# The output stage of a two-layer state-space kernel: how the column-wise scans are added in, and on which engines the norm's sums run

## The chip, the cores and the metric

The kernel runs on one core of one Trainium2 chip. The metric is the device time of one execution in microseconds (us); the time of a kernel is the median of its runs. A profile of one further execution gives the trace from which single durations come.

## What is computed

The input is a batch of four 128x128 images with 192 channels, float32. Layer 0 (projection, depthwise convolution, one scan over the pixels, three dilated convolutions, a norm, an output projection) is not touched. Layer 1 is a two-dimensional selective scan: the image is projected, convolved, and scanned in four orders k = 0 to 3 (by rows forward and backward, by columns forward and backward). What matters here comes after the scans:

```python
y0 = ys[0].reshape(B, C, H, W)
y1 = ys[1][..., ::-1].reshape(B, C, H, W)
y2 = jnp.transpose(ys[2].reshape(B, C, W, H), (0, 1, 3, 2))
y3 = jnp.transpose(ys[3][..., ::-1].reshape(B, C, W, H), (0, 1, 3, 2))
y = y0 + y1 + y2 + y3
y = jnp.transpose(y, (0, 2, 3, 1))
mu = y.mean(-1, keepdims=True)
var = y.var(-1, keepdims=True)
y = (y - mu) / jnp.sqrt(var + 1e-05) * ln_g + ln_b
y = y * jax.nn.silu(z)
return y @ out_w
```

So the column-wise results have to be turned (width and height exchanged) before they meet the row-wise ones; then come a norm over the 192 channels of each pixel, a gate with silu(z), and an output projection. z is a projection of the layer's input, which is also added to the result.

## The kernel before

Four stages follow each other: the transposition of the input, layer 0, the convolution of layer 1 (`in_conv`, whose lines L933 to L959 the prediction also reads), the scans (`scans`), and the output stage (`outputs`). In layer 1 two images form a pair (PAIRS = 2), and their 2 x 192 channels lie in three blocks of 128 partitions: block 0 holds channels 0 to 127 of the first image, block 2 those of the second, block 1 the last 64 channels of both, one image in each half. A chunk is 8 image rows, T = 1024 pixels; there are 16 chunks (NCH) for each pair.

**The order of the work.** Each stage writes its operations to a list (`op`) with an engine, an assumed cost, what they read and write, and for some a shift in the list (`early`). `Order.emit` plays the list through once at build time, with these costs, and so fixes the order of the instructions on each engine; the engines then keep that order and wait for one another where data or buffers ask for it. `keep` is the penalty for an operation that needs another activation table than the one loaded, `idle` the wait that is accepted before another operation is preferred. A buffer (`buf(tag, bufs, ...)`) names its ring and how many tiles the ring has.

**The scans.** For each pair, each order k and each chunk there are six groups m of 64 channels with eight units each. A unit is an exponential on ACT (`dA`, L1244), a scan on DVE (L1250), a product on POOL (`hc`, L1256) and a matmul that sums over states (`Y`, L1264). After eight units `finish` adds the sum to what the earlier order left (`prev`; L1286, L1290 or L1292 by k) and stores it: `y[0]` holds the row-wise sum, `y[1]` the column-wise sum, whose pixels are in column order. There is one `Y` bank and there are two `y` tiles.

**The output stage** has two parts. `merge(p, i)` loads a whole 128x128 image of the column-wise block (`img`, L1377, four parts of 2 MB), then for each chunk loads the row-wise block (`m`, L1384), adds the turned view of the image to it on DVE (L1388, reading `img` with a step of one column) and stores the sum back (L1394). All three blocks of pair 0 are merged ahead of its first chunk; those of pair 1 are placed at chunks 1, 6 and 11 of pair 0. `chunk(p, j)` does the rest for 8 rows:

- load three y blocks (L1403) and three blocks of the layer's input (`x`, L789);
- average over channels on PE (`averages`): for each of two images a 128-row matmul (L1424) and a 64-row matmul for its half of block 1 (L1429), into a PSUM tile of two banks. It is called twice, first for the mean (called M here), then for the mean square (V);
- subtract the mean on DVE (L1437), square on ACT (L1441), V, then Ln (L1446) and Exp (L1450) on ACT give the reciprocal root;
- scale by it on DVE (the norm, L1453);
- for each block project the input to z (`pair_project`, L828), Silu on ACT (L1462), add the bias and gate on DVE (L1465);
- the output projection O in two halves of four image rows: 128-row matmuls with the gated y (L1479) and with an identity for the input itself (L1482), then the 64-row ones (L1488, L1493), row by row; ACT copies the result out (`ot`, L1500) and SP stores it (L1505).

PSUM holds three tiles `f` for averages and O and one tile `z`. y and x have two tiles for each block, the squares `s` one, the output `ot` one for each image. POOL has no work in this stage. 64-row matmuls on the two halves of the partitions [...]can run side by side; a block's matmuls here alternate between 128-row and 64-row form.

Of the kernel before, what the change touches and what calls it, by code (L numbers as in the profile page):

```python
# [16 lines left out]
B, H, W, C = 4, 128, 128, 192  # L17
L = H * W
R = 8
# [24 lines left out]
DILS = (5, 3)  # L44
NEAR = [(t, t // 3 - 1, t % 3 - 1) for t in range(9) if t != 4]
# [37 lines left out]
class Order:  # L83
# [32 lines left out]
    def emit(self):  # L116
# [14 lines left out]
        while len(order) < len(ops):  # L131
# [55 lines left out]
            for m in after[n]:  # L187
                left[m] -= 1
                ready_at[m] = max(
                    ready_at[m], done + (0.0 if e == ops[m][0] and not size else self.HOP)  # L190
                )
                if not left[m] and m < high:
                    ready[ops[m][0]].append(m)
        for n in order:
            for b in ops[n][4]:
                b()
            ops[n][2]()
# [3 lines left out]
class Maker:  # L201
# [784 lines left out]
    def scans(self, xc, delta, cs, y, w, ident, alog, dsum, dtb2):  # L986
# [22 lines left out]
        with ExitStack() as ctx:  # L1009
# [261 lines left out]
            def finish(m):  # L1271
# [12 lines left out]
                def add():  # L1284
                    if k == 0:
                        nc.vector.scalar_tensor_tensor(  # L1286
                            t(), prev[m](), dsum[:, hf : hf + 1], ym(), ALU.mult, ALU.add
                        )
                    elif k == 2:
                        nc.vector.tensor_copy(t(), ym())  # L1290
                    else:
                        nc.vector.tensor_tensor(t(), prev[m](), ym(), ALU.add)  # L1292

                def store():
                    for th, a in enumerate(y_part(y[k // 2][p][i], m)):
                        nc.sync.dma_start(a, t()[64 * th : 64 * th + 64])
# [55 lines left out]
    def outputs(self, y, x1T, gn, out, win, wo, vec, ident, eps):  # L1352
# [4 lines left out]
        with ExitStack() as ctx:  # L1357
            p1 = ctx.enter_context(tc.tile_pool(name="s_1", bufs=1))
            ps = ctx.enter_context(tc.tile_pool(name="s_ps", bufs=3, space=PSUM))
            psZ = ctx.enter_context(tc.tile_pool(name="s_psZ", bufs=1, space=PSUM))  # L1360
# [3 lines left out]
            od = Order(keep=167, idle=1.550, rate=300e3)  # L1364
            op = od.op

# [3 lines left out]
            def bank2(stream):  # L1370
                return buf("f", 3, 128, 2, 512, pool=ps, stream=stream)

            def merge(p, i):
                img = buf("img", 1, 128, W, H)
                for c in range(4):
                    ws = slice(c * W // 4, (c + 1) * W // 4)
                    op("SP", 0.1, lambda ws=ws: nc.sync.dma_start(  # L1377
                        img()[:, ws].rearrange("p w h -> p (w h)"),
                        y[1][p][i][:, ws.start * H : ws.stop * H],
                    ), reads=[img], writes=[(img, c)], size=2.1e6, early=-243)  # L1380
                for j in range(NCH):
                    cols = slice(j * T, (j + 1) * T)
                    t = buf("m", 3, 128, T)
                    op("SP", 0.11, lambda t=t, cols=cols: nc.sync.dma_start(  # L1384
                        t(), y[0][p][i][:, cols]), writes=[t], size=524e3, early=-438)

                    def add(t=t, j=j):
                        nc.vector.tensor_tensor(  # L1388
                            rows(t()), rows(t()),
                            img()[:, :, R * j : R * (j + 1)].rearrange("p w r -> p r w"), ALU.add,  # L1390
                        )

                    op("DVE", 1.9, add, reads=[img, *((img, c) for c in range(4))], writes=[t], early=-723)
                    op("SP", 0.12, lambda t=t, cols=cols: nc.sync.dma_start(  # L1394
                        y[0][p][i][:, cols], t()), reads=[t], writes=[("y", p, i, j)], size=524e3, early=-216)

            def chunk(p, j):
                terms, bias = pw[p]
                cols = slice(j * T, (j + 1) * T)
                ys, x1, sq = [], [], []  # L1400
                for i in range(3):
                    yt, xt = buf(f"y{i}", 2, 128, T), buf(f"x{i}", 2, 128, T)
                    op("SP", 0.1, lambda yt=yt, i=i: nc.sync.dma_start(yt(), y[0][p][i][:, cols]),  # L1403
                       reads=[("y", p, i, j)], writes=[yt], size=524e3, early=765)
                    op("SP", 0.13, lambda xt=xt, i=i: self.load_block(xt(), x1T, p, i, cols),
                       writes=[xt], size=524e3)
                    ys.append(yt)
                    x1.append(xt)
                    sq.append(buf(f"s{i}", 1, 128, T))
# [7 lines left out]
                def averages(name, src):  # L1417
                    gs = [bank2(name), bank2(name)]

                    def mm():  # L1420
                        for h in range(2):
                            c = slice(512 * h, 512 * h + 512)
                            for e in range(2):
                                nc.tensor.matmul(  # L1424
                                    gs[e]()[:, h], avg, src[2 * e]()[:, c], start=True, stop=False
                                )
                            for e in range(2):
                                k = slice(64 * e, 64 * e + 64)
                                nc.tensor.matmul(  # L1429
                                    gs[e]()[:, h], avg[k], src[1]()[k, c], start=False, stop=True  # L1430
                                )

                    op("PE", 4.4, mm, reads=src, writes=gs, early=57)
                    return gs

                gm = averages("M", ys)
                by_batch(lambda e, i, k: op("DVE", 1.23, lambda: nc.vector.tensor_tensor(  # L1437
                    ys[i]()[k], ys[i]()[k], flat(gm[e]())[k], ALU.subtract),
                    reads=[gm[e]], writes=[ys[i]]))
                for i in range(3):  # L1440
                    op("ACT", 1.08, lambda i=i: nc.scalar.activation(sq[i](), ys[i](), AF.Square),  # L1441
                       reads=[ys[i]], writes=[sq[i]])
                gv = averages("V", sq)
                rs = [buf("rs", 2, 128, T) for _ in range(2)]
                for e in range(2):
                    op("ACT", 1.13, lambda e=e: nc.scalar.activation(  # L1446
                        rs[e](), flat(gv[e]()), AF.Ln, bias=eps),
                        reads=[gv[e]], writes=[rs[e]], table="ln")
                for e in range(2):
                    op("ACT", 1.1, lambda e=e: nc.scalar.activation(  # L1450
                        rs[e](), rs[e](), AF.Exp, scale=-0.5),
                        writes=[rs[e]], table="exp")
                by_batch(lambda e, i, k: op("DVE", 1.24, lambda: nc.vector.scalar_tensor_tensor(  # L1453
                    ys[i]()[k], ys[i]()[k], vec[k, i % 2, V1_G : V1_G + 1], rs[e]()[k],
                    ALU.mult, ALU.mult), reads=[rs[e]], writes=[ys[i]], early=-540))
                for i in range(3):
                    gz, sz = buf("z", 1, 128, 2, 512, pool=psZ), buf("sz", 2, 128, T)
                    op("PE", 3.0, lambda i=i, gz=gz: self.pair_project(
                        [gz()[:, h] for h in range(2)], i, terms,
                        lambda src, h: x1[src]()[:, 512 * h : 512 * h + 512],  # L1460
                    ), reads=x1, writes=[gz])
                    op("ACT", 1.05, lambda i=i, gz=gz, sz=sz: nc.scalar.activation(  # L1462
                        sz(), flat(gz()), AF.Silu, bias=bias[:, i : i + 1]),
                        reads=[gz], writes=[sz], table="silu")
                    op("DVE", 1.25, lambda i=i, sz=sz: nc.vector.scalar_tensor_tensor(  # L1465
                        ys[i](), ys[i](), vec[:, i % 2, V1_B : V1_B + 1], sz(),
                        ALU.add, ALU.mult), reads=[sz], writes=[ys[i]])
                ot = [buf(f"ot{e}", 1, 128, R, C) for e in range(2)]
                for h in range(2):
                    go = [bank2("O"), bank2("O")]  # L1470

                    def mm(h=h, go=go):
                        for r in range(4):
                            tok = slice((4 * h + r) * W, (4 * h + r + 1) * W)
                            dst = [
                                go[e]()[:, r // 2, (r % 2) * C : (r % 2 + 1) * C] for e in range(2)
                            ]
                            for e in range(2):
                                nc.tensor.matmul(  # L1479
                                    dst[e], ys[2 * e]()[:, tok], wo[:, 0], start=True, stop=False  # L1480
                                )
                                nc.tensor.matmul(  # L1482
                                    dst[e][:, 0:128], x1[2 * e]()[:, tok], ident,
                                    start=False, stop=False,
                                )
                            for e in range(2):
                                k = slice(64 * e, 64 * e + 64)
                                nc.tensor.matmul(  # L1488
                                    dst[e], ys[1]()[k, tok], wo[k, 1 + e], start=False, stop=False
                                )  # L1490
                            for e in range(2):
                                k = slice(64 * e, 64 * e + 64)
                                nc.tensor.matmul(  # L1493
                                    dst[e][:, 128:C], x1[1]()[k, tok], ident[k, k],
                                    start=False, stop=True,
# [210 lines left out]
```

## Time and profile before

| what | value |
|---|---|
| median of 3 runs | 26036.89 us (26029.69 to 26136.25) |
| the profiled execution | 26124.05 us, span 26122.3 us |
| busy in the span: PE, DVE, ACT, POOL | 91%, 84%, 80%, 79% |
| output stage, first image load to the end | 24528 to 26122 us |
| DVE merge add, L1388, 128x1024 | 96 times, mean 1.92 us |
| DVE subtraction L1437, norm L1453, gate L1465 | mean 1.21, 1.28, 1.28 us |
| ACT square, Ln, Exp, Silu, copy to `ot` | mean 1.05, 1.11, 1.05, 1.11, 0.80 us |
| ACT table load | mean 1.28 us |

The page gives busy time over the whole span; the groups by line give how often an instruction ran and how long one took; the chain of waits follows the work that ended last back from the end; the order of time lists single instructions. A row of the groups or of the order of time names line, engine, operation, output and inputs. A float32 matmul appears as two records. "Granted clock" is the share of TensorE's full clock.

### The profile page before, as it was taken

The page shows a single profiled execution, that of the slowest core. Times are in us where ns is not written, and L with a number is a line of the kernel's source. Part 1 is how long each engine was busy: PE and PEld are TensorE (multiplying, and loading weights), DVE is VectorE, ACT ScalarE, POOL GpSimd, SP SyncE. Part 2 cuts the span into 40 slices and gives each one's busy share as a digit, 9 for nine tenths or more (in the row PEclk, how much of TensorE's full clock was granted, in tenths as well). Part 3 has the DMA queues.
Part 4 walks back from the last instruction along what each step waited for, and adds up shares of the span by engine and source line. Part 5 has one row for each costly group of instructions (what it writes and reads, how often), then busy time and mean ns, then how long its engine had stood idle before and what let it go on. Part 6 is the DMA issues. An engine that isn't in the chain of part 4 may idle for free.

```text
span 26122.3 us, 435536 instructions
## 1 busy us (share of the span) xinstructions
PE 23658.7 (91%) x168196; PEld 8704.1 (33%) x168196; DVE 21934.3 (84%) x15400; ACT 20802.7 (80%) x24211; POOL 20539.1 (79%) x9962
## 2 busy tenths in 40 slices
PE   4999999998899999999999999999999999999699
PEld 2333232322233333333333333333333333333245
DVE  3889888888788989888898889888988898888643
ACT  5999998966688888888887878888888888888443
POOL 3999998955588888888888888888888888888400
PEclk6999999999899999999998989999999999999799
DMA  6998889876545455444444545444544444544563
GB/s 205 248 248 251 245 249 244 248 213 208 155 127 134 131 136 136 131 124 120 122 126 127 134 124 137 129 129 132 135 132 132 116 124 118 134 128 130 189 229 107
DMA packets 1646421, 4171.84 MB, mean 160 GB/s; under 512 B 236800, under 2 KB 387776, under 8 KB 1641280
## 3 DMA queue, kind: packets, MB, share of 16 engines
q1 hardware_dynamic: 1644352, 4143.97, 57.0%
q8 instruction: 1333, 21.84, 0.4%
q14 instruction: 736, 6.03, 0.1%
HBM read 3203.95 MB, written 939.10 MB: 159 GB/s over the span
## 4 chain that ended last, share of the span: by engine, by line
PE 43%; DVE 19%; ACT 12%; issue 6%; DMA 4%; POOL 4%; SPq 1%; DVEq 0%; POOLq 0%; ACTq 0%
DVE h L1250 14%; PE f L1217 13%; PE Y L1264 10%; ACT h L1228 6%; ACT dA L1244 3%; PE s L1071 3%; PE hf L615 3%; POOL hc L1256 2%; PE s L1094 2%; PE z L828 1%; DMA C<-cs 1%; DVE D L1143 1%; DVE acc L939 1%; PE f L723 1%; PE g L706 1%
## 5 line engine op out<-in xcount | busy, mean ns | idle before, releaser
L1256 POOL TENSOR_TENSOR hc<-h,C 128x1024 f32<-128x1024 f32 x6144 | 14344.0, 2366 | 2340.8 <-PE Y L1264 1133.0
L1250 DVE TENSOR_TENSOR_SCAN h<-dA,st,h 128x1024 f32<-128x1024 f32 x5760 | 13128.7, 2331 | 746.4 <-ACT st L1280 300.2
L1228 ACT COPY h<-f 128x1024 f32<-128x1024 f32 (+3 forms) x8192 | 6334.4, 799 | 2176.4 <-PE f L1217 2109.6
L1217 PE MATMUL f<-D,dT 32*64 32x256 f32 x98304 | 7138.7, 407 | 782.8 <-ACT h L1228 638.0
L1264 PE MATMUL Y<-hc,sel 128*64 128x512 f32 x24576 | 6967.1, 654 | 477.1 <-POOL hc L1256 222.0
L1244 ACT ACTIVATE dA<-d,alog 128x1024 f32<-128x1024 f32 x6144 | 6904.6, 1124 | 308.8 <-DVE h L1250 254.3
L1217 PEld LDWEIGHTS f<-D,dT 32*64 32x64 f32 x98304 | 3270.7, 137 | 6657.9 <-ACT h L1228 4793.7
L495 POOL TENSOR_TENSOR xs<-xs,pr 128x1024 f32<-128x1024 f32 x1536 | 3641.6, 2373 | 233.5 <-ACT pr L490 160.4
L635 DVE SCALAR_TENSOR_TENSOR hf<-hh,vec,hf 128x512 f32<-128x512 f32 x3072 | 2315.2, 754 | 232.2 <-PE hf L615 134.3
L1264 PEld LDWEIGHTS Y<-hc,sel 128*64 128x64 f32 x24576 | 1318.8, 141 | 2971.1 <-issue 1794.2
L615 PE MATMUL hf<-sa,diag 96*32 96x512 f32 x18432 | 2173.9, 610 | 78.8 <-DVE y L646 40.3
L1143 DVE TENSOR_TENSOR D<-s,mask 128x1024 f32<-128x1024 f32 x1024 | 1238.2, 1209 | 865.4 <-PE s L1137 865.4
L490 ACT ACTIVATE pr<-xi,vec 128x1024 f32<-128x1024 f32 x1536 | 1703.7, 1142 | 174.6 <-POOL xs L495 171.7
L615 PEld LDWEIGHTS hf<-sa,diag 96*32 96x32 f32 x18432 | 553.4, 110 | 1599.4 <-issue 1340.0
L1104 POOL TENSOR_TENSOR u<-l,u 128x1024 f32<-128x1024 f32 x384 | 908.4, 2366 | 164.7 <-ACT l L1097 139.2
L1250 DVE TENSOR_TENSOR_SCAN h<-dA,h 128x1024 f32<-128x1024 f32 x384 | 856.5, 2273 | 63.6 <-ACT dA L1244 31.4
L1094 PE MATMUL s<-pj,w 128*128 128x512 f32 x1536 | 901.3, 670 | 6.3 <-ACT l L1097 2.0
L1097 ACT ACTIVATE l<-s,vec 128x512 f32<-128x512 f32 x768 | 528.0, 687 | 345.2 <-PE s L1094 340.7
L1071 PE MATMUL s<-u,w 128*128 128x512 f32 x1536 | 743.2, 621 | 53.8 <-DMA prev<-xc 53.0
L706 PE MATMUL g<-xz,w 96*128 96x512 f32 x1536 | 764.2, 622 | 26.6 <-DVE y L715 14.0
L1137 PEld LDWEIGHTS s<-ident,pj 128*128 128x128 f32 x4096 | 550.0, 195 | 595.0 <-issue 255.1
L939 DVE SCALAR_TENSOR_TENSOR acc<-xi,vec,acc 128x1024 f32<-128x1024 f32 x384 | 715.9, 1864 | 26.9
(208 smaller groups left out, 21228.3 us busy)
## 6 DMA issues: line engine op xcount, KB each, us to landing
C<-cs SPq DMA_DIRECT2D x4096, 256.0 KB, 4.8
sa<-hpad SPq DMA_DIRECT2D x2304, 276.0 KB, 6.2
d<-delta SPq DMA_DIRECT2D x1536, 256.0 KB, 4.2
u<-xc SPq DMA_DIRECT2D x384, 512.0 KB, 4.7
delta<-l SPq DMA_DIRECT2D x384, 512.0 KB, 3.8
y<-y SPq DMA_DIRECT2D x1536, 128.0 KB, 3.3
hh<-hpad SPq DMA_DIRECT2D x384, 414.0 KB, 6.3
hpad<-hp SPq DMA_DIRECT2D x192, 552.0 KB, 6.7
```

What stands on the lines that cost most here:

```text
L490: op("ACT", 1.1, lambda pr=pr, t=t: nc.scalar.activation(rows(pr()), x()[:, t // 3 : t // 3 + R, t % 3 : t % 3 + W], AF.Copy, scale=v(k, V ...
L495: op("POOL", 2.38, lambda pr=pr: nc.gpsimd.tensor_tensor(o(), o(), pr(), ALU.add), reads=[pr], writes=[o], early=-390)
L615: nc.tensor.matmul(o()[32 * g : 32 * g + 32], diag[:, d, s, k, g], x[:, g, :, c0 : c0 + W], start=(d == 0 and s == 0), stop=(d == 1 and s ...
L635: nc.vector.scalar_tensor_tensor(o3, hh()[:, 1 + dy : 5 + dy, PAD + dx : PAD + dx + W], v(k, V0_K + col), o3, ALU.mult, ALU.add,)
L1071: nc.tensor.matmul(g(), wt()[:, 0, i], uu[i]()[:, 512 * c : 512 * c + 512], start=(i == 0), stop=(i == 2),)
L1143: nc.vector.tensor_tensor(t().rearrange("t a (n s) -> t (a n) s", s=32), g()[:, : 2 * NS].unsqueeze(2).to_broadcast([128, 2 * NS, 32]), ma ...
L1217: nc.tensor.matmul(gs()[64 * jn : 64 * jn + 64, n, 256 * a : 256 * a + 256], td()[rt, r // 64, 2 * sb + a], tD()[rt, a, 256 * jn : 256 * j ...
L1228: nc.scalar.copy(H[:, at : at + nq, 256 * sb : 256 * sb + 256].rearrange("p q (a r s) -> p q a r s", a=2, s=32)[:, :, :, 2 * rp : 2 * rp + 2],
L1244: op("ACT", 1.16, lambda: nc.scalar.activation(a(), d(), AF.Exp, scale=alog[:, c : c + 1]), reads=[d], writes=[a], table="exp", early=-522)
L1250: nc.vector.tensor_tensor_scan(hs[:, way], a()[:, way], hs[:, way], 0.0 if at == 0 else s0()[:, q : q + 1], ALU.mult, ALU.add,)
L1256: op("POOL", 2.4, lambda: nc.gpsimd.tensor_tensor(t(), hs, tC(), ALU.mult), reads=[hq, tC], writes=[t])
L1264: nc.tensor.matmul(ym()[64 * th : 64 * th + 64], sel, t()[:, 512 * th : 512 * th + 512], start=(q == 0), stop=(q == NQ - 1),)
```

## The change

The edit has five parts, four of them in the output stage.

1. **Turned groups.** For k = 3 (the last of the column orders) `finish` writes its sum in another order: within each tile the four columns of 128 pixels are split in four groups of TG = 32 image rows, and the store goes to a new scratch tensor `yt`, laid out by group, then column, then row. A store has 256 runs of 512 bytes instead of 64 of 2 KB.
2. **Addition chunk by chunk.** `merge` and `img` are gone. Every fourth chunk loads for each block the next 32-row group of `yt` (2 MB, ring of two); each chunk loads its y blocks from `y[0]` as the scans left them, and DVE adds the turned view of the group in place. There is no write-back.
3. **Norm sums partly on GpSimd.** POOL adds block 1's half to block 0 or block 2 (64 partitions by 1024), and copies the other half, ahead of M; it adds the squares likewise ahead of V. Each average is then 128-row matmuls alone, two for each image.
4. **Paired matmuls.** The z projections of blocks 0 and 2 are issued together, first all 128-row ones, then the 64-row ones of both images in pairs; block 1's projection is as before. O likewise: in each half first all 128-row matmuls of four rows, then all 64-row ones. PSUM has four `f` tiles and no `z` tile.
5. **New list order.** A subclass `Timed` of `Order` makes the list with other costs, a model of the TensorE clock, of the change of tiling mode and of the way between engines, and with shifts by kind of operation (`OUT_EARLY`) in place of the shifts at each operation.

The order of all instructions ahead of the output stage is the same as before, but for the form of the add and the store of part 1.

```diff
+TG = 32
+OUT_KEEP, OUT_IDLE = 520, 2.009
+OUT_EARLY = {'oh': -4, 'ln': 51, 'o': -32, 'ot': -4, 'silu': -9, 'turned': -50, 'V': -3, 'out': -74, 'x': -130, 'merge': 32, 'sum': -42, 'sqs': -157, 'rs': -137, 'norm': -8, 'gate': 343}
...
+class Timed(Order):
+    WINDOW, LOW, HIGH, DRAIN = 3.41333, 0.355, 0.74, 0.165
+    AFTER = {"PE": 0.237, "ACT": 0.105, "DVE": 0.088, "POOL": 0.055, "SP": 0.0}
...
+            if e == "PE":
+                m, area = extra[n]
+                if m != mode:
+                    at = max(at, free[e] + self.DRAIN)
+                    mode = m
+                end, work = at, cost
+                while work > 1e-9:
+                    while edge <= end:
+                        share, used = used / self.WINDOW, 0.0
+                        warm = share >= self.LOW if warm else share > self.HIGH
+                        edge += self.WINDOW
+                    need = min(edge - end, work if warm else 2 * work)
+                    used += need * area
+                    end += need
+                    work -= need if warm else need / 2
...
 # scans, finish(m)
+                        nc.vector.tensor_tensor(
+                            t().rearrange("c (g w h) -> c g w h", g=IH // TG, h=TG),
+                            *(
+                                x.rearrange("c (w g h) -> c g w h", g=IH // TG, h=TG)
+                                for x in (prev[m](), ym())
+                            ),
+                            ALU.add,
+                        )
...
+                        w0 = TG * (R * j + 4 * th)
+                        nc.sync.dma_start(
+                            yt[p][i][r : r + 64].rearrange("c (g n) -> c g n", g=IH // TG)[
+                                :, :, w0 : w0 + 4 * TG
+                            ],
+                            src.rearrange("c (g n) -> c g n", g=IH // TG),
+                        )
...
 # outputs
-            ps = ctx.enter_context(tc.tile_pool(name="s_ps", bufs=3, space=PSUM))
-            psZ = ctx.enter_context(tc.tile_pool(name="s_psZ", bufs=1, space=PSUM))
+            ps = ctx.enter_context(tc.tile_pool(name="s_ps", bufs=4, space=PSUM))
...
-            od = Order(keep=167, idle=1.550, rate=300e3)
+            od = Timed(OUT_EARLY, keep=OUT_KEEP, idle=OUT_IDLE, rate=270e3)
...
+            def load_turned(p, g, i):
+                t = turned[i] = buf(f"g{i}", 2, 128, W, TG)
+                n = W * TG
+                op("SP", 0.1, lambda: nc.sync.dma_start(
+                    t().rearrange("p w h -> p (w h)"), yt[p][i][:, g * n : (g + 1) * n]
+                ), writes=[t], size=2.1e6, rank="turned")
...
+                    op("DVE", 1.9, lambda yi=yi, tg=tg: nc.vector.tensor_tensor(
+                        rows(yi()), rows(yi()),
+                        tg()[:, :, h0 : h0 + R].rearrange("p w r -> p r w"), ALU.add,
+                    ), reads=[tg], writes=[yi], rank="merge")
...
-                            for e in range(2):
-                                k = slice(64 * e, 64 * e + 64)
-                                nc.tensor.matmul(
-                                    gs[e]()[:, h], avg[k], src[1]()[k, c], start=False, stop=True
-                                )
...
+                def pool_add(out, a, b, k, rank):
+                    op("POOL", 2.31, lambda: nc.gpsimd.tensor_tensor(
+                        out()[k], a()[k], b()[k], ALU.add), reads=[a, b], writes=[out], rank=rank)
+
+                sums = [buf(f"s{2 * e}", 1, 128, T) for e in range(2)]
+                for e, (mine, rest) in enumerate(((LOW, HIGH_), (HIGH_, LOW))):
+                    pool_add(sums[e], ys[2 * e], ys[1], mine, "sum")
+                    op("POOL", 1.4, lambda e=e, rest=rest: nc.gpsimd.tensor_copy(
+                        sums[e]()[rest], ys[2 * e]()[rest]),
+                        reads=[ys[2 * e]], writes=[sums[e]], rank="sum")
+                gm = averages("M", sums)
...
+                pool_add(sq[0], sq[0], sq[1], LOW, "sqs")
+                pool_add(sq[2], sq[2], sq[1], HIGH_, "sqs")
+                gv = averages("V", [sq[0], sq[2]])
...
+                op("PE", 3.41, whole, reads=[x1[0], x1[2]], writes=g02, claims=sz[:2],
+                   rank="z")
+                op("PE", 1.71, halves, reads=[x1[1]], writes=g02, mode="64x128", rank="zh")
+                for e, i in enumerate((0, 2)):
+                    gate(i, g02[e], sz[e])
...
+                gate(1, g1, sz[2])
...
+                    op("PE", 4.27, whole, reads=[ys[0], ys[2], x1[0], x1[2]], writes=go, rank="o")
+                    op("PE", 1.71, halves, reads=[ys[1], x1[1]], writes=go, mode="64x128",
+                       rank="oh")
```

In the order that comes out, the queues of a regular chunk run as follows. PE: V(n+1), z(n+1), M(n+2), O(n+1). DVE: the four subtractions of n+1, the three merge adds of n+2, the norms and gates of n+1. POOL: the square sums of n+1, the sums of n+2. SP: y(n+2), the stores of n, x(n+2). At every fourth chunk the groups are loaded between x and y, and PE issues both 128-row parts of O ahead of both 64-row parts and M after them.

## The prediction

> **What bounds the kernel now.** I read the page first: TensorE is busy 91% of the 26122.3 us, but that mean covers stages that the change does not touch. So I asked for the output stage alone. Its first image load is issued at 24528 us and the kernel ends at 26122: 1594 us, 6% of the whole. The table of busy time by stretch (columns: stretch, its length, busy us with instruction counts on PE, weight load, DVE, ACT, POOL, then granted clock, DMA share, GB/s):
>
> ```profile
> 24540.00:24640.00 100.00, 13.41 (x22) 3.23 (x22) 30.08 (x16) 3.35 (x3) 0.00 (x0) 0.55 0.92 340
> 24900.00:25000.00 100.00, 93.04 (x426) 51.98 (x424) 56.14 (x39) 38.02 (x37) 0.00 (x0) 0.97 0.78 258
> 25600.00:25700.00 100.00, 95.68 (x452) 52.15 (x452) 30.11 (x25) 41.47 (x41) 0.00 (x0) 1.00 0.40 115
> ```
>
> Two regimes. First DMA rules while PE is almost idle (13 of 100 us): the whole-image merge of `y[1]` into `y[0]` must run before any chunk; the first output matmul (L1479) is at 24773, 245 us into the stage. Then PE is 93 to 96% busy at full clock while POOL does nothing. In the chain of waits of that second part the two stores of every second chunk stand at
>
> ```profile
> 25413.10 8.15 DMA out<-ot
> ...
> 25498.39 8.44 DMA out<-ot
> ...
> 25583.87 8.30 DMA out<-ot
> ```
>
> that is 85.4 us for two chunks, **42.7 us a chunk**. The PE pieces of a chunk in the same chain:
>
> ```profile
> 25437.31 4.22 PE z L828 x8
> 25441.53 1.91 PE f L1424 x4
> 25443.44 1.06 PE f L1429 x4
> ...
> 25447.47 4.13 PE z L828 x12
> ```
>
> One average is 2 x (1.91 + 1.06) = 5.94 us, two a chunk; the z projections are 4.22 + 4.13 + 4.29; an O half is 4 rows of 1.98 us (in the order of time a row is 1.30 us of 128-row matmuls and 0.69 us of paired 64-row ones). Sum 11.9 + 12.6 + 15.9 = 40.4 us of PE, so 2.3 us are gaps. PE bounds the steady part.
>
> **What the Trainium skill says.** TensorEngine Tiling (Array Packing), Key Properties: changing the tiling mode drains TensorE. The trace agrees: four records of 128x512 take 1.91 us, where a record is 0.43 us apart from the next inside a run (4 x 0.43 = 1.71), so a change costs about 0.2 us. SBUF — State Buffer, Who interferes with whom: a VectorE instruction with two SBUF inputs and a GpSimd instruction that reads SBUF exclude each other for the whole instruction. This trace agrees, in the layer-1 convolution:
>
> ```profile
> 6407.90 1.27 DVE L939 SCALAR_TENSOR_TENSOR acc<-xi,vec,c 128x1024 f32<-128x1024 f32 x1
> 6408.11 2.35 POOL L957 TENSOR_TENSOR acc<-acc,pr 128x1024 f32<-128x1024 f32 x1 [3.93 <-issue]
> 6409.21 8.34 DVE L939 SCALAR_TENSOR_TENSOR acc<-xi,vec,acc 128x1024 f32<-128x1024 f32 x4
> 6410.50 3.25 POOL L955 TENSOR_TENSOR pr<-pr 128x1024 f32<-128x1024 f32 x1
> ```
>
> Four DVE taps of 1.285 us (5.1 us) take 8.34, and POOL's 2.35 us add is recorded as 3.25: they take turns. TensorE: Matmul & The Clock Gate, What's actually happening: an idle window of about 3.4 us halves the clock; the 0.55 in the idle stretch above agrees. DMA: Bandwidth & Descriptors, Specifications: 512 B is the least transfer at line rate; no run here shows 512 B runs by themselves.
>
> **The change, part by part.**
>
> *Scans.* 192 finishes with k = 3 read both inputs of an add with permuted strides and store 256 runs of 512 B twice instead of 64 of 2 KB twice; the queue order there is unchanged. The add (L1292) takes 0.67 us. A strided read costs at most what the merge shows, 1.92 against 1.21 us, so +0.4 us each, 77 us if all of it held the single `Y` bank's next matmul; below, zero or a hair less. The stores land in 3.2 us with two `y` tiles and some 22 us between finishes, so they hide; DMA is 48% busy there. I take +5 us, ends -5 and +80.
>
> *Merge at the head.* 24 image loads, 96 `m` loads and 96 write-backs (216 issues on SP, 150 MB) go; 24 loads of 2 MB groups come. The first chunk now needs 1.57 MB of y and 6.3 MB of groups: at the 300 to 340 GB/s of the first row, 25 us. Then merge (1.9), two sums on POOL (7.5), M (3.6), subtractions (5), Square and two POOL adds (6), V (4), Ln/table/Exp (4), norm and gate (10), O (13), some of it overlapped and PE cold: first O done about 88 us into the stage. Before, by the same yardstick, 1594 - 31 x 42.7 - 8 (last store) = 262 us. **174 us saved.**
>
> *PE per chunk.* M and V lose their 64-row matmuls and most drains: 3.4 to 3.6 each. z for the two full blocks: 3.4, the paired halves 1.7 + 0.2, z1 stays 4.1. O: per half 4 x 1.07 + 4 x 0.43 + two drains of 0.24 = 6.5, twice. Sum 3.6 + 3.4 + 1.9 + 4.1 + 3.6 + 13.0 = **29.6 us** for 40.4. If PE still bound, that would be the period.
>
> *What comes beside it.* DVE: three merges 5.8, four subtractions 4.9, four norms 5.1, three gates 3.85 = 19.6 us. POOL (64 rows by 1024; nearest row 128x1024, 2.36 us, and I find no price by rows, so the same; a copy 1.2 to 2.4, I take 1.4): 4 x 2.36 + 2 x 1.4 = 12.2 us. Neither reaches 29.6 alone. But merges, norms and gates (14.8 us) read two SBUF operands and exclude POOL's 12.2. Only the subtractions (one operand in PSUM) are free. ACT's work stays: three squares 3.2, two Ln 2.2, two Exp 2.1, three Silu 3.3, four copies 3.2, three table loads 3.85 = 17.9 us; DMA moves 6.3 MB a chunk, 21 us at 300 GB/s. Both stay under PE's 29.6; without that cover DMA would be the next to bind, at 21.
>
> *The loop.* The new queue orders are: PE V(n+1), Z, zh, z1, M(n+2), O(n+1); DVE sub(n+1), merge(n+2), norm/gate(n+1), sub(n+2); POOL sums(n+2), then square sums(n+2). y has two buffers, so y(n+2) loads when O(n) lets go. Count from the end of O(n): y0 (let go 2 us sooner), y1, y2 land at 1.5, 4 and 5 to 6 (three loads: 3.3 to 5.7 us in this stage); merges end 7.8; then POOL and DVE in turns: sum 10.2, norm 11.5, copy 12.9, norm 14.2, sum 16.6, gate 17.9, copy 19.3, norm 20.6, gate 21.9, norm 23.1, gate 24.4. O(n+1) needs the second gate: 22.0, not 16.7 where PE would be ready. Its second half needs the M banks, let go by the four subtractions: 24.4 + 4.9 = 29.3; then 6.4 us: 35.7. Square, the `ot` copies between, and two POOL adds end at 36.1, just in time for V. So about 35.7 us, and PE stands idle some 4 us in one piece before M's second half, which the clock rule charges at half speed for a window: +1 to 2. **Period 37 us** (35 to 40). Every fourth chunk the groups' 6.3 MB (some 20 us of DMA) hold y behind them; PE runs both wholes of O before the halves there, and by the same count two such cycles give 71 us, no more than two regular ones. SP has room: 9 issues a chunk at 0.3 to 1 us.
>
> *Sum.* Stage after: 88 + 31 x 37 + 8 = 1243 us, saving 351; with +5 for the scans, 346. The profiled execution took 26124.05 (span 26122.3), 87 us above the median 26036.89 and inside the timed 26029.69 to 26136.25; I take the saving off the median: 26037 - 346 = **25690**.
>
> **The rivals.** (A) Turns cost little (POOL's work falls into DVE's subtractions and waits, or 64 rows are quicker): PE binds at about 30. Stage 88 + 31 x 30 + 35 for bumps every fourth chunk + 8 = 1061, saving 533: 25504. For it: 29.6 fits all in-order counts when each engine runs freely. Against it: L939 and L955. (B) Turns and half clock feed each other: a cold PE stretches O, y leaves later, period 41 to 42: saving about 200, 25840. For it: 0.55 at the head; against it: O is long and dense. (C) Slower: the permuted 512 B stores at L1296's place back up SP, and C loads (256 KB in 4.7 us) behind them starve POOL's multiply, for the 32 of 128 steps with k = 3. It decides at 346/192 = 1.8 us lost per finish; +0.5% needs 2.5, thus 26170. Against it: 48% DMA and unchanged bytes. (D) The new stage does not overlap as written and gives everything back: period 48, no difference; nothing in the orders suggests it.
>
> **How the numbers follow.** Main case 0.74, A 0.14, B 0.07, C 0.02, D 0.03. The main case spans periods 35 to 40: 25628 to 25783, and the launch spread of +-50. The range 25500 to 25820 takes in half of A and a little of B. A measurement here can tell about 0.5% (130 us) from nothing: faster 0.95, same 0.03, slower 0.02.
>
> **What would show it.** In the profile after: the stage near 1240 us; PE 78 to 84% busy in its steady part, 29 to 31 us a chunk; merge, norm and gate rows with means well above 1.92 and 1.28, or POOL adds above 2.36, while the subtraction stays 1.21; y-to-O waits on the gate. Rows at their old means and PE above 93% would prove A. A longer scan stage (the head later than 24528) would prove C. If the DVE and POOL rows stretch and the period is still 30, my in-order count is wrong.

## The result and the profile after

| | before | changed |
|---|---|---|
| median of the launches | 26033.29 us | 25643.96 us |
| ratio | | 0.9841 (95% interval 0.9813 to 0.9868) |
| profiled execution, span | 26122.3 us | 25609.2 us |
| output stage in the profile, first group (image) load to the end | 24528.1 to 26122.3 = 1594 us | 24437.6 to 25609.2 = 1172 us |
| first store of `ot` after the stage's start | 271.7 us | 71.3 us |
| from there to the end | 1322.6 us | 1100.3 us |

The forecast was 25690 us, in the range 25500 to 25820. The stage lost 422 us, 200 at its head and 222 in its loop. The lines behind these lengths (count, duration in ns, first and last start), two of before and two of the changed kernel:

```profile
L1377 SPq DMA_DIRECT2D img<-y x24: 320/437/1347, 24528.1 to 25204.4; - x24
L1505 SPq DMA_DIRECT2D out<-ot x64: 372/389/1852, 24799.7 to 26115.7; - x64
...
L1528 SPq DMA_DIRECT2D g<-yt x24: 320/392/655, 24437.6 to 25265.1; - x24
L1693 SPq DMA_DIRECT2D out<-ot x64: 372/389/678, 24508.9 to 25602.2; - x64
```

The two profiled spans differ by 513, because the part ahead of the stage also varies: its length was anywhere from 24331 to 24558 us in the profiles of this study, and the instruction order of that part is the same in all of them. So below the length of the stage in one profile is compared, and the ratio stands beside it where there are enough launches.

The table of busy time by stretch of the changed kernel (stretch, length, busy us and counts on PE, weight load, DVE, ACT, POOL, then granted clock, DMA share, GB/s):

```profile
24437.00:24530.00 93.00, 66.70 (x258) 37.58 (x259) 51.16 (x39) 33.05 (x31) 34.47 (x16) 0.78 0.69 254
...
24800.00:24900.00 100.00, 91.71 (x514) 59.42 (x514) 66.38 (x41) 46.57 (x47) 40.11 (x17) 0.98 0.67 219
```

The DMA-only head is gone: PE has 67 us of work in the first 93. From 24600 to 25500 us PE is 86 to 93% busy, less than before, and POOL, idle before, is 36 to 50% busy. The granted clock of these stretches, 0.95 to 0.98, is a mean: in stretches of 4 us it is 1.00 in most and falls as low as 0.50 behind some of PE's waits, mostly in the pairs of chunks in which a new group begins. PE's busy time multiplied by the missing share of the clock, stretch by stretch, adds up to some 27 us after the head (an estimate from these figures). The stores of four chunks, from the order of time of the SP queue (start, duration):

```profile
24826.94 1.09 SPq L1693 DMA_DIRECT2D out<-ot  x2
24860.54 1.09 SPq L1693 DMA_DIRECT2D out<-ot  x2
24892.82 1.09 SPq L1693 DMA_DIRECT2D out<-ot  x2
24936.27 1.09 SPq L1693 DMA_DIRECT2D out<-ot  x2
```

A regular chunk takes about 33.5 us (33.6 here); the pair in which a new group begins 32.3 + 43.5. From the first store to the end it is 1100.3/31 = 35.5 us a chunk, for 42.7.

The groups of DVE and POOL in 24700 to 25500 us (line, engine, operation, output and input, shapes, count, busy us, mean ns, then idle before them):

```profile
L1547 DVE TENSOR_TENSOR y<-y,g 128x1024 f32<-128x1024 f32 x66 | 139.2, 2151 | 102.0 <-DMA y<-y 97.7 <-PE f L1565 4.2
L1611 DVE SCALAR_TENSOR_TENSOR y<-y,vec,sz 128x1024 f32<-128x1024 f32 x68 | 118.3, 1740 | 9.5 <-ACT sz L1608 4.5 <-DVE y L1603 0.5
L1603 DVE SCALAR_TENSOR_TENSOR y<-y,vec,rs 128x1024 f32<-128x1024 f32 x45 | 91.5, 2034 | 116.5 <-ACT rs L1600 116.4
L1584 DVE TENSOR_TENSOR y<-y,f 128x1024 f32<-128x1024 f32 x46 | 55.8, 1213 | 38.9 <-PE f L1565 38.4
L1574 POOL TENSOR_TENSOR s<-y,y 64x1024 f32<-64x1024 f32 x44 | 148.2, 3369 | 165.3 <-DVE y L1547 156.3 <-issue 4.9 <-PE f L1565 4.1
L1580 POOL COPY s<-y 64x1024 f32<-64x1024 f32 x45 | 78.1, 1735 | 2.0
```

The gate went from 1.28 to 1.74 us, the norm from 1.28 to 2.03 (1.72 on 64 rows), the merge from 1.92 to 2.15. The subtraction, whose second operand lies in PSUM, is still 1.21. This is what taking turns would look like; e6 below tests it. One regular chunk in the order of time shows the turns themselves:

```profile
24829.88 3.83 DVE L1547 TENSOR_TENSOR y<-y,g 128x1024 f32<-128x1024 f32 x2 [1.21 <-DMA y<-y]
24832.07 3.87 POOL L1574 TENSOR_TENSOR s<-y,y 64x1024 f32<-64x1024 f32 x1 [5.47 <-DVE y L1547]
...
24833.89 5.11 DVE L1603 SCALAR_TENSOR_TENSOR y<-y,vec,rs 128x1024 f32<-128x1024 f32 x2 [0.18 <-ACT rs L1600]
...
24841.26 1.93 POOL L1580 COPY s<-y 64x1024 f32<-64x1024 f32 x1
...
24843.24 1.98 PE L1565 MATMUL f<-s,avg 128*128 128x512 f32 x4 [2.13 <-POOL s L1580]
24844.37 1.28 DVE L1611 SCALAR_TENSOR_TENSOR y<-y,vec,sz 128x1024 f32<-128x1024 f32 x1
```

V of this chunk begins at 24826.0. Two norms that need 2.6 us are spread over 5.1; PE stands 2.1 us ahead of M's second half, waiting for POOL's copy. PE's waits over 24700 to 25500, longest first (what waited, for what: us, times, longest):

```profile
PE f L1565 <- POOL s L1580: 32.6, 17, 3.8
PE f L1565 <- POOL s L1574: 19.8, 8, 5.7
PE f L1658 <- DVE y L1611: 15.0, 11, 2.4
PE f L1670 <- DVE y L1611: 12.1, 5, 2.4
```

M and V wait for POOL (52 us), O for the gate (27 us): the two doors that the forecast named.

### The profile page after: what moved, and what is told of

The parts are those of the page before. It is cut to its first block, busy times and chain, and to the rows that moved or that the text cites. A ratio compares the mean times of both kernels' runs of the same rounds, so it can differ in the third digit from the quotient of the medians.

```text
span 25609.2 us, 434783 instructions
## 1 busy us (share of the span) xinstructions
PE 23256.1 (91%) x167684; PEld 8620.0 (34%) x167684; DVE 22073.4 (86%) x15400; ACT 20799.2 (81%) x24211; POOL 21019.5 (82%) x10154
```

## The experiments

"Stage" is the length as in the table; ratios are to the kernel before.

| run | what | stage us | regular period us | ratio (95%) |
|---|---|---|---|---|
| before | | 1594 | 42.7 | |
| changed | | 1172 | 33.5 | 0.9841 (0.9813 to 0.9868) |
| e11 | changed, again | 1170 | 33.5 | 0.9845 (0.9823 to 0.9867) |
| e1 | part 1 alone | 1588 | 42.7 | 0.9987 (0.9974 to 1.0001) |
| e10, e13 | parts 3 and 4 undone | 1325, 1324 | 40.35 | e13: 0.9900 (0.9874 to 0.9926) |
| e7 | grouping of averages and O alone | 1483 | 39.4 | 0.9951 (0.9915 to 0.9987) |
| e2 | no exclusion, POOL fills longer | 1139 | 33 to 35 | 0.9825 (0.9789 to 0.9861) |
| e6 | no exclusion, POOL fills as long | 1090 | 31.8 | |
| e3 | mean on PE | 1105 | 32.5 | 0.9817 (0.9794 to 0.9840) |
| e5 | part 4 undone | 1346 | 38.8 to 40.6 | 0.9921 (0.9896 to 0.9946) |
| e8 | no shifts in the list | 1345 | 41.0 | |
| e9, e12 | mean on PE, z1 grouped | 1096, 1097 | 32.15 | e12: 0.9787 (0.9769 to 0.9805) |

**Part 1 alone (e1_scans_only).**

```diff
 # before, with scans() of the changed kernel
-    mk.scans(xc, delta, cs, y, w, ident, alog, dsum, dtb2)
+    mk.scans(xc, delta, cs, y, yt, w, ident, alog, dsum, dtb2)
```

> The kernel before with the scans of the changed kernel: the k = 3 sums are added with permuted strides and stored to yt in 512-byte runs, which nothing reads; the output stage is that of before and therefore lacks the k = 3 sums. Theory (the new stores and the strided add are free): ratio to before 1.000 within 0.3%, the k = 3 add at 0.66 us, stores landing in 3 to 4 us, output stage 1594 us. Rival (the 90 us by which the profiled scans of the changed kernel were shorter come from part 1): about 26030 - 90 = 25940, with the gain in the two k = 3 passes. Rival (part 1 costs): slower by up to 80 us.

Measured: ratio 0.9987, stage 1588 us. The k = 3 add in the groups of DVE (first the permuted one, then k = 1), and the last line of the answer on the store's line:

```profile
L1296 DVE TENSOR_TENSOR y<-prev,Y 128x512 f32<-128x512 f32 x192 | 128.2, 668 | 52.3 <-PE Y L1266 52.2
L1294 DVE TENSOR_TENSOR y<-prev,Y 128x512 f32<-128x512 f32 x192 | 128.1, 667 | 34.7 <-PE Y L1266 34.6
...
DMA to landing us min/median/max: 2.3/3.3/7.4
```

Runs of 32 elements cost DVE nothing, and 512-byte runs land in the 3.3 us of the 2 KB ones. Part 1 costs nothing that these runs can tell. A gain of the 90 us by which the changed kernel's profile reached the stage sooner would be a ratio of 0.9965, below the interval, so they do not come from it.

**No exclusion (e2_no_exclusion, e6_no_exclusion_short).**

```diff
+                def fill(x, *ns):
+                    for n in ns:
+                        nc.gpsimd.memset(x[:, :n], 0.0)
...
-                        out()[k], a()[k], b()[k], ALU.add), reads=[a, b], writes=[out], rank=rank)
+                        nc.gpsimd.tensor_tensor(out()[k, 0:8], a()[k, 0:8], b()[k, 0:8], ALU.add)
+                        fill(out()[k], T, T, 512)   # e6: T, T
...
+                        nc.gpsimd.tensor_copy(sums[e]()[rest, 0:8], ys[2 * e]()[rest, 0:8])
+                        fill(sums[e]()[rest], T)
```

> The changed kernel with every POOL add and copy of the output stage replaced by one on 8 columns (same inputs, so the same waits) followed by memsets that fill the time; the mean and the variance are therefore not computed. POOL is busy as long, but reads SBUF only for some 0.1 us. Theory (DVE and POOL take turns, and this sets the loop): merge, norm and gate rows fall back to about 1.92 and 1.28 us, the regular period from 33.5 to about 30 us, PE over 95% busy; the stage about 100 us shorter than the 1172 of the changed kernel. Rival (turns are covered anyway; latency of loads sets the loop): period 33 to 33.5, stage within 20 us of 1172.

In e2 the DVE rows fell back as expected, but the period stayed at 33 to 35. The expectation failed, and the edit was at fault: a fill of 2.5 us and a small read made POOL's add 2.8 us instead of 2.36, and the small reads still had to wait for their turn, so PE waited for POOL ahead of M as before (2.45 us in one chunk). e6 shortens the fill and nothing else.

> As e2_no_exclusion, with the fills shortened so that a POOL add and its copy take 3.4 us together when nothing holds them, as in the changed kernel; in e2 they took 4.0, and M's second half still waited for POOL. The mean and variance are not computed. Theory (taking turns sets the regular loop through two doors, the gate and POOL's sums): with the sums no longer late, the regular period falls to the sum of PE's work, 30.6 to 31.5 us, and PE's wait for POOL ahead of M nearly goes. Rival (the regular loop hangs on loads and on the chain through Square, not on turns): 33 us or more, as in e2.

Groups of e6 in 24800 to 25500, and PE's first two waits there:

```profile
L1547 DVE TENSOR_TENSOR y<-y,g 128x1024 f32<-128x1024 f32 x63 | 121.0, 1957 | 123.5 <-DMA y<-y 120.8 <-PE f L1565 2.5
L1621 DVE SCALAR_TENSOR_TENSOR y<-y,vec,sz 128x1024 f32<-128x1024 f32 x63 | 80.9, 1285 | 19.9 <-ACT sz L1618 15.3 <-DVE y L1613 0.5
L1613 DVE SCALAR_TENSOR_TENSOR y<-y,vec,rs 128x1024 f32<-128x1024 f32 x42 | 53.8, 1281 | 110.9 <-ACT rs L1610 110.9
```

```profile
PE f L1565 <- POOL s L1575: 22.2, 17, 1.9
PE f L1668 <- DVE y L1621: 11.1, 8, 1.5
```

Merge 1.96, gate and norm 1.28; PE 665 us busy of 700; period 31.8 and the stage 81 us shorter than the changed kernel's. POOL is about as long busy (286 of 700 us, 306 in the changed kernel) but hardly reads SBUF, and 1.7 of the 2.9 us between PE's work (30.6, below) and the period go. So exclusion is most of what holds the loop there. The remaining wait for POOL (22 us in 21 chunks) I put down to its plain length and the turns of the small reads; no run separates these.

**Mean on PE (e3_mean_on_pe), and z1 grouped (e9_mean_on_pe_z1, e12_best_again).**

```diff
-                sums = [buf(f"s{2 * e}", 1, 128, T) for e in range(2)]
...
-                gm = averages("M", sums)
+                gm = averages_pe("M", ys)
...
 # e9 and e12, block 1's z
-                op("PE", 3.58, lambda: self.pair_project(
+                def middle():
+                    for h in range(2):
+                        nc.tensor.matmul(
+                            g1()[:, h], of[1][1], x1[1]()[:, 512 * h : 512 * h + 512],
+                            start=True, stop=False,
+                        )
+                    for h in range(2):
+                        for src, m in ((0, slice(0, 64)), (2, slice(64, 128))):
...
```

`averages_pe` issues the 128-row matmuls of both images on blocks 0 and 2, then the 64-row ones on the halves of block 1 in pairs.

> The changed kernel with part 3 undone for the mean alone: M is 128-row matmuls on blocks 0 and 2, then paired 64-row matmuls on block 1; POOL keeps the two adds of squares. PE grows by 1.7 + 0.2 us a chunk to 31.5, POOL loses 7.5 us. Theory (turns set the loop): period about 32 us, stage some 40 to 60 us shorter than the changed kernel's. Rival (PE is the bound): 1.9 x 32 = 60 us longer.

Period 32.5, stage 67 us shorter than the changed kernel's. Its stretch 24700 to 25500 and all of PE's waits in it:

```profile
24700.00:25500.00 800.00, 785.05 (x4359) 488.14 (x4358) 461.80 (x337) 415.29 (x409) 116.01 (x50) 1.00 0.57 182
```

```profile
PE f L1579 <- issue: 8.5, 5, 1.7
PE f L1579 <- ACT sz L1626: 6.4, 5, 1.3
```

PE is 98% busy at full clock: PE has 1.9 us more work a chunk, POOL 6.8 us less of sums and copies, and the kernel is faster. The slow stretches of the clock, some 27 us of the stage in the changed kernel, are gone as well. This excludes rival A, under which e3 would have been slower. In this loop PE binds, so fewer changes of mode should show:

> e3_mean_on_pe, and block 1's z projection grouped as well: its two 128-row matmuls first, then the four 64-column ones in pairs. e3 is bound by PE (98% busy, period 32.5 us). Theory: two changes of tiling mode go, 0.4 us a chunk, stage about 13 us shorter than e3's 1105; against before a ratio of about 0.981. Rival: no change, because the wait moves to ACT or DVE.

Period 32.15, stage 1096: 0.35 us a chunk, 8 us in all where 13 were expected. The launches beside e9 scatter by over 100 us, so both were run again on one chip.

> The changed kernel once more, beside e12 on the same chip. Expected: stage 1172 us within 10 in the profile, regular period 33.5 and every fourth 43 to 46; ratio to before 0.984 within 0.003. If the stage differs by more than 20 us, single profiles can't be compared as they are here.

> e9_mean_on_pe_z1 once more, against e11 on the same chip. Theory: the stage is 1096 within 10 us, 75 us shorter than the changed kernel's, so its ratio to before is 0.003 lower than e11's. Rival: in the launches nothing of the 75 us is seen, because PE at 98% busy lowers the clock.

Stages 1170 and 1097; ratios 0.9845 and 0.9787, median 25493.05 us for e12 against 25667.11 for e11. e12 is faster than both kernels. The difference between the ratios is 0.006 where the stage gives 0.003. In the two profiles the part ahead of the stage differs as well (24558 us in e11, 24434 in e12); why is not shown.

**Part 4 undone (e5_rows).**

```diff
-                op("PE", 1.71, halves, reads=[x1[1]], writes=g02, mode="64x128", rank="zh")
+                for i in (0, 2, 1):
+                    gz = bank2("Z")
+                    op("PE", 4.2, lambda i=i, gz=gz: self.pair_project(
+                        [gz()[:, h] for h in range(2)], i, terms,
...
-                    op("PE", 4.27, whole, reads=[ys[0], ys[2], x1[0], x1[2]], writes=go, rank="o")
+                    op("PE", 7.94, mm, reads=[*ys, *x1], writes=go, rank="o")
```

> The changed kernel with part 4 undone: z block by block and O row by row as before, 64-row matmuls between the 128-row ones. PE grows by 3.2 (z) + 2.9 (O) us a chunk to about 35.7. Theory (turns set a loop of 33.5 us that holds O and not z): z's growth hides until PE binds, so the period becomes about 36.5 to 37 us; stage 90 to 120 us longer than 1172. Rival (PE binds in the changed kernel): 6.1 x 32 = 195 us longer. Rival (DVE and POOL alone bind): no change.

Measured: stage 174 us longer, period 38.8 to 40.6: too much for the theory and nearer to the rival's 195, for z's growth did not hide (that PE binds the changed kernel, as the rival has it, e3 excludes). Three things show in the order of time. First, the loads of the next y are issued 1.3 us before V in place of 3.0, and the first merge starts 2.3 us after V in place of 0.7, the second 5.7 in place of 3.9. Row by row, O reads the y tiles of blocks 0 and 2 until its last row; grouped, it lets them go some two microseconds before it ends. So the grouping also shortens the loop at the buffer. Second, O's first row now holds 64-row matmuls on block 1 and waits 1.8 us for the third gate. Third, O itself takes some 16 us in place of 13.8. A chunk at full clock, 24860.2 to 24899.0, is 38.8 us: some 36 us of PE's work, 1.1 of waiting for POOL's copy and 1.8 for that gate. In the next, of 40.5 us, one row of O behind the same wait takes 3.5 us in place of 2.0, at half speed: that is the difference between 38.8 and 40.6.

**One part alone (e7_pairs_only; e10_merge_only and e13_merge_only_again).** In e7's averages (and alike in O) the loops are exchanged:

```diff
-                        for h in range(2):
-                            c = slice(512 * h, 512 * h + 512)
-                            for e in range(2):
+                        for e in range(2):
+                            for h in range(2):
...
+                        for h in range(2):
                             for e in range(2):
                                 k = slice(64 * e, 64 * e + 64)
```

> The kernel before with the grouping of part 4 alone, for the averages and for O: all 128-row matmuls first, then the 64-row ones in pairs; z and everything else as before. Theory (PE binds the kernel before in its steady part): PE loses 2 x 0.4 us in the averages and 2 x 1.0 us in O, so two chunks take about 79.7 us in place of 85.4, and the stage is some 85 us shorter than 1594. The merge at its head is not touched and keeps its 245 us. Rival (the store of ot or the single z tile sets the pace): below 20 us.

Two chunks took 78.7 us for 85.4 (79.7 expected), the stage 111 us less. In e10 averages, z and O have the forms of before and POOL no work (e5's edit, and the averages likewise):

```diff
-                sums = [buf(f"s{2 * e}", 1, 128, T) for e in range(2)]
...
-                gm = averages("M", sums)
+                gm = averages("M", ys)
...
-                gv = averages("V", [sq[0], sq[2]])
+                gv = averages("V", sq)
```

> The changed kernel with parts 3 and 4 undone: averages, z and O on PE in the forms of before, no POOL work; the turned groups, the addition chunk by chunk and the Timed list stay. Theory: only the head goes. First stores of ot about 75 us into the stage in place of 272 (24799.7 - 24528.1), then PE binds with 40.4 us of work, period 41 to 43 us: stage about 75 + 31 x 42 + 8 = 1385, some 210 us shorter than before; ratio about 0.992. Rival (the old regime hid the write-back and the head's DMA is merely spread out): period above 44 and stage above 1450.

```profile
24800.00:25500.00 700.00, 700.00 (x3174) 364.97 (x3172) 332.60 (x242) 315.99 (x308) 0.00 (x0) 1.00 0.47 151
```

PE has no gap at all: period 40.35, the sum of its work. The first store comes 91 us into the stage, 181 sooner than before, and the 2.3 us of gaps a chunk are gone (whether by the list order or because the merges of pair 1 no longer fall into the loop was not separated). That is 270 of the 422 us, more than the 210 expected. Its two launches gave 0.9854, more than 270 us explain, hence:

> e10_merge_only once more, since its two launches were 0.985 of before while its stage in the profile was 1325 us, 153 us longer than the changed kernel's 1172. Theory (the stage is what counts, and the part ahead of it varies from launch to launch by some 100 us either way): stage 1325 within 10 us, ratio to before about (26038 - 270)/26038 = 0.990. Rival (the launches of this kernel are shorter ahead of the stage as well): ratio 0.985 again.

0.9900, as the stage says. Parts 3 and 4 together bring the other 153 us. Since e3, with the mean on PE, is 67 us shorter still, the use of POOL for the mean costs more than it saves here.

**No shifts (e8_no_shifts).**

```diff
-OUT_EARLY = {'oh': -4, 'ln': 51, 'o': -32, 'ot': -4, 'silu': -9, 'turned': -50, 'V': -3, 'out': -74, 'x': -130, 'merge': 32, 'sum': -42, 'sqs': -157, 'rs': -137, 'norm': -8, 'gate': 343}
+OUT_EARLY = {}
```

> The changed kernel with part 5's shifts taken away (OUT_EARLY empty), the costs and the model of Timed kept, so only the order of the list differs. Theory: the order matters as far as it keeps M(n+2) and Z ahead of O while POOL works; without it PE waits for more of the chain, period 36 to 42 us, stage 80 to 250 us longer than 1172. Rival (orders are irrelevant because buffers force them): within 20 us.

Period 41.0, stage 173 us longer, within the expected band. PE's longest waits in 24800 to 25500:

```profile
PE f L1658 <- DVE y L1611: 83.3, 36, 4.2
PE f L1565 <- POOL s L1574: 60.6, 34, 3.3
```

The same two doors, wider: 8.4 us a chunk for these waits, where the four lines of the changed kernel above give 3.5. Behind the wait for the gate the clock falls too (0.64 in 25006 to 25010 us, behind a wait of 4.2 us); counted as above this is some 1.6 us a chunk. Without its shifts the changed kernel loses 173 us, more than the 153 that parts 3 and 4 bring.

## Why the prediction was right

- **Head.** Forecast 174 us (88 against 262), measured 200 (71.3 against 271.7). The steps were right, both ends a little off. The first store came 17 us sooner than the count had O done: POOL's sums ran between the landing groups and were through 25.7 us into the stage (24463.3), where the count of loads, merge and sums gives 34. The head of before was 10 us longer than its yardstick gave.
- **PE's work.** Forecast 29.6 us, measured about 30.6: e3 is bound by PE at 32.5, of which 1.9 are the mean's 64-row matmuls. The term that was too small is O. In the chain of waits of the changed kernel one half runs

```profile
25565.28 0.52 PE f L1658 x2
...
25569.86 1.50 PE f L1670 x16
25571.36 0.84 PE f L1676 x16
25572.20 1.93 PE f L1565 x4
```

  from 25565.28 to 25572.20 = 6.92 us, not 6.5.
- **The turns.** They set the loop, as forecast, and with them M waits for POOL and O for the gate. Counted from the start of V (24826.0), forecast and measured: merges end 7.8 and 7.7, first copy ends near 12.9 and 12, second gate 21.9 and 19.6, third gate 24.4 and 22.3, O ends 35.7 and 33.6. The 2 us came off between the first sum and the second gate: a POOL copy is 1.03 us where it runs free, not 1.4, and the other turns were each a little shorter than counted; why is not shown.
- **Clock.** In the regular chunk the 1 to 2 us for a half-speed window did not come: PE's gap there was 2.1 us, and the granted clock from 24826 to 24860 us was 1.00. So the regular period was 33.5, not 37. It came in the chunks with a new group instead, as the next point shows, behind a wait no longer than this one. What decides between the two is not shown.
- **Fourth chunk.** Forecast no dearer than two regular ones (71 us for two); measured 30.6 to 32.3 + 43.5 to 46.2, some 7 to 11 us over two of 33.5. This step failed, in two ways. One is the turns, which fall there between merges and square sums: in 24892 to 24915 the three merges (5.8 us) take 9.94 and the two square sums (4.77) take 6.99, and V waits 2.0 and 1.3 us for POOL, where my count let one end before the other. The other is the clock, which was left out of the count for these chunks. V runs slow behind its waits:

```profile
24902.97 2.73 PE L1565 MATMUL f<-s,avg 128*128 128x512 f32 x4 [2.03 <-POOL s L1574]
...
24906.98 3.78 PE L1565 MATMUL f<-s,avg 128*128 128x512 f32 x4 [1.27 <-POOL s L1574]
```

  where four records take 1.98 us in the regular chunk; the granted clock is 0.58 in 24902.9 to 24910.6. Just before, O's 64-row parts waited 2.4 us for the gate and then lost 1.7 us in the same way (0.74 in 24885.5 to 24892.0). So in this pair of chunks (24859.6 to 24935.4) PE's waits are 9.6 us, where two regular ones have some 5, and the slow stretches cost about 4 more: each is about half of the excess. Without exclusion (e6) the long chunk is still 40.5 to 42.3, behind one of 28.1. In one of 42.3 V waits 1.9 and 1.2 us for POOL's square sums and some 2.6 us go to slow matmuls. e3, without POOL's sums of the mean and at full clock, has 35.8.
- **Sum.** 346 us forecast, 389 between the medians and 422 in the stage. The two errors in the period (too much for turns and clock in a regular chunk, too little for every fourth) cancel in part, which is luck: 37 forecast, 35.5 measured on the mean. The stage came out 71 us shorter than forecast (1172 for 1243): 55 of them lie behind the first store, 17 ahead of it. One sign also missed: PE is 86 to 93% busy in stretches of 100 us, not 78 to 84, since its work is longer and the chunk shorter than counted.
- **Rivals.** A needed a period of 30 with PE binding and the rows at their old means: the rows stretched, and e3 and e6 exclude it. C (the 512-byte stores): e1 excludes it. B (turns and half clock feed each other) came in part, in every fourth chunk, and not as a period of 41 to 42. D did not come.

## What to carry to other kernels

Before work is moved to an idle engine, ask what it reads there and whose reads it will hold up. GpSimd's adds and copies stretched VectorE's two-operand work from 14.8 to some 19 us a chunk, and its sums for the mean came out dearer than 1.9 us more on the engine that was called the bottleneck. Ask also what the waits do to the clock: in the changed kernel half speed behind waits cost some 27 us of the stage, and with the mean on PE nothing after its head. When a pass over the whole image must end before a pipeline can start, let the producer store the layout that the consumer reads in pieces; here the turned store cost nothing and the first result came 181 us sooner (e10). And the order in which matmuls read a tile decides when its buffer comes free and which input they wait for first: grouping them by form saved the mode changes, some two microseconds of load latency in the loop and a wait of 1.8 us for the third gate.

## What the runs showed of the hardware that I had not expected

- VectorE reads runs of 32 float32 elements, strided in SBUF and in PSUM, at the contiguous rate: 0.668 against 0.667 us for 128x512 (e1). The merge, which reads single elements 128 bytes apart, took 1.96 us where nothing blocked it (e6), about as much as before at 512 bytes apart (1.92).
- A GpSimd copy of 64x1024 takes 1.03 us free and a two-operand add of the same size 2.34 to 2.36, the same as on 128 partitions (2.35, L957 of the kernel before).
- Even a GpSimd add on eight columns takes longer beside VectorE's two-operand instructions: 1.06 us on the mean for the sums of e6, where it is 0.19 when free.
- A wait of 2.1 us in a regular chunk left PE at full clock, while one of 2.0 us in a fourth chunk was followed by matmuls at half speed (four records in 2.73 and 3.78 us, 1.98 at full clock).
